# ScalarE sums the moments of the layernorms beside the scans, and the last batch's out_proj weights are loaded early into buffers of u

## The chip, the cores and the metric

The kernel runs on one core of one Trainium2 chip. The metric is the device time of one execution in microseconds. Three runs of the kernel before took 1672.40, 1673.51 and 1674.71 us; the median is 1673.51 us. Its engines are called PE (TensorE), DVE (VectorE), ACT (ScalarE), POOL (GpSimd) and SP (SyncE, which here only issues DMAs). Each engine works through its own instructions in the order in which the program gives them; semaphores make one engine wait for another.

## The reference, cut to what matters

One decoder layer on 4 batches of 512 tokens of width 512: a Mamba block with a selective scan (1024 channels, 16 states each), a cross attention that consists of two SmoothQuant int8 products, and a mixture of 16 experts (top 2) with a shared expert. Each of the three is added to the residual, and each is preceded by a layernorm without weights:

```python
def _layernorm(x, axis=-1, eps=1e-05):
    m = jnp.mean(x, axis=axis, keepdims=True)
    v = jnp.var(x, axis=axis, keepdims=True)
    return (x - m) / jnp.sqrt(v + eps)

def step(h, inputs):                      # the scan, 512 steps
    d_t, B_t, C_t, u_t = inputs
    dA = jnp.exp(d_t[..., None] * A)
    h = h * dA + (d_t * u_t)[..., None] * B_t[:, None, :]
    y = jnp.einsum('bdn,bn->bd', h, C_t)
    return (h, y)

x = x + mamba(_layernorm(x))              # ends with out_proj: einsum('md,bld->blm', out_proj_weight, y)
x = x + quant(_layernorm(x), fside, ctx)
x = x + moe(_layernorm(x))
```

## The kernel before

**The work.** A batch has 4 tiles of 128 tokens. There are three layernorms for each tile, so 4 x 3 x 4 = 48 layernorms of 128 x 512. Each is done by three helpers: `ln_stats` (L327, L328: bn_stats and bn_aggr on DVE give mean and variance), `ln_scale` (L335 to L337: three operations of 128 x 1 on POOL give 1/sqrt(v + eps) by a power, and minus the mean times that) and `ln_scaled` (L341: one ACT activation applies both to the tile).

**The scans.** A batch has 8 groups of 128 channels (`c`), and each group 8 units (`n`), so a batch has 64 slots and the kernel 256. In a slot ACT makes two exponentials of 128 x 512 (L663, into one of two PSUM buffers `da`), POOL one product `bu` of 128 x 1024 (L665, two buffers), DVE the scan over 128 x 1024 (L672) and the product with C (L678), and PE sums over the states into `py` (L690). DVE's L712 multiplies by the gate and writes the result over `u`, which is what out_proj reads; the group is then entered in `self.done` as ("gated", b, c). The `rep` copies (L650, SP) spread delta and delta times u over the partitions for L663 and L665.

**What runs beside them.** Three generators give the rest of the work in steps, each step a few instructions:

- `front(b)` for batches 1 to 3: `layernormed` (first layernorm and transposes), in_proj, convolution, gates, x_proj. All fronts must be over before the scans of batch 3 begin.
- `back(b)`: the out_proj weights `wout` are loaded (L730, eight DMAs of 256 KB, two to a step, into a pool of their own), then the tiles of `x` (L737); out_proj (L742), the addition to `x` (L752), the second layernorm; two quantized products (`quant_linear`); the addition (L787), the third layernorm; `moe_front` with routing (L1110) and the shared expert (L1052, L1060, L1084), whose last addition is L1090. The backs of the four batches follow one another in one generator. Batch 2's back may start only when all fronts are done, so with slot 192; batch 3's needs its own scans and runs after them, apart from its first six channel groups of out_proj, which need only ("gated", 3, 5).
- `experts(group 0)`, the experts for the tokens of batches 0 and 1: sorting, then up to 31 tiles, each with two gathers issued by POOL (L1175 weights, L1419 tokens), transposes (L346), products (L1450, L1465) and a store (L1473). They begin with batch 3's scans and go on after them, beside batch 3's back. The second group begins after batch 3's routing and ends the kernel.

**The planner.** The order of every engine's instructions is fixed when the program is built. `Pace` keeps a modelled time for each engine. In each slot `scan_batch` calls `more` three times: before the scan, between scan and product, and after it. Each call offers every generator two steps. A step is written if the tiles and engines that the generator named with its last `yield` are free by the model, with some tolerance. A generator that lags behind its due count gets a larger tolerance, LATE = 100 ns for each step that it is late; the due count is BACK_STEPS, or FRONT_STEPS, for every DUE = 58 slots. After the scans a loop writes whichever generator is ready first, with a preference for the back.

```python
BACK_STEPS, FRONT_STEPS, DUE, LATE = 164, 112, 58, 100
backs.due = lambda slot: BACK_STEPS * (slot - NC * NU) / DUE
def go_if_clear(self, due=0):
    if not self.over and self.pace.clear(self.wait, max(0, due - self.written) * LATE):
        self.go()
```

`staged(items, *stages)` pipelines: in one step the stages of several items are written, the latest stage first, so that item t is in stage s while item t+1 is in stage s-1. One more stage makes the pipeline one step longer.

**Buffers of u.** The pool `us` holds 17 buffers of 128 x 512 under the tag "u", given out in turn. Batch 0 takes 8, batch 1 takes 4 (its other 4 lie elsewhere), batches 2 and 3 take 8 each; the end of the kernel takes more of them for the results. A tile that gets an old buffer waits until the last reader of that buffer is through.

Of the kernel before, what the change touches and what calls it, by code (L numbers as in the profile page):

```python
# [19 lines left out]
P = 128  # L20
# [22 lines left out]

BACK_STEPS, FRONT_STEPS, DUE, LATE = 164, 112, 58, 100
FIRST = 2000
# [224 lines left out]
class Kernel:  # L270
    def __init__(self, ctx, tc, args):
# [24 lines left out]
        nc.sync.dma_start(self.gate_sb, self.gatew)  # L296
        T = B * NT
        self.idf = const.tile([P, T, 2], F32, name="idf")
        self.topw = const.tile([P, T, 2], F32, name="topw")

# [14 lines left out]
        self.last = None  # L315
        self.ws = {}
        self.skips, self.u_of = {}, []
        self.started = set()
        self.table = False

    def ln_stats(self, x):
# [35 lines left out]
    def layernormed(self, b, sb, bank, xnT):  # L359

        nc = self.nc
        xs, ln, tp = {}, {}, {}

        def load(t):
            xs[t] = sb.tile([P, DM], F32, name="xin", bufs=4)
            nc.sync.dma_start(xs[t], self.x[b, t * P : (t + 1) * P, :])

        def stats(t):
            ln[t] = self.ln_stats(xs[t])
            return ln[t]  # L370

        def scale(t):
            ln[t] = self.ln_scale(ln[t])
            return ln[t]

        def scaled(t):
            self.ln_scaled(xs[t], xs[t], ln[t])
            return xs[t]

        def turn(t):  # L380
            tp[t] = bank.take([P, NK, P])
            self.transposes(tp[t], xs[t], NK)
            return tp[t]

        def turned(t):
            nc.scalar.copy(xnT[:, :, t * P : (t + 1) * P], tp[t])
            bank.done(tp[t])

        for t in range(NT):
            load(t)  # L390
        yield xs[0]
        yield from staged(range(NT), stats, scale, scaled, turn, turned, bank=bank)

# [323 lines left out]
    def back(self, b, G):  # L717
# [6 lines left out]
        with ExitStack() as outer:  # L724
            keep = outer.enter_context(tc.tile_pool(name=f"keep{b}", bufs=1, reuse_waits="tile", side="right"))
            xn = keep.tile([P, NT, DM], F32, name="xn")
            with tc.tile_pool(name=f"out{b}", bufs=2, reuse_waits="tile", side="right") as sb:
                wout = sb.tile([P, NC, DM], F32, name="wout", bufs=1)
                for c in range(NC):
                    nc.sync.dma_start(wout[:, c, :], self.wout[:, c, :])  # L730
                    if c % 2:
                        yield
                xr, po, ln = {}, {}, {}

# [4 lines left out]
                def product(t):  # L739
                    po[t] = G.take([P, DM])  # L740
                    for c in part:
                        nc.tensor.matmul(  # L742
                            po[t],
                            st["u"][c][:, t * P : (t + 1) * P],
                            wout[:, c, :],
                            start=(c == part[0]),
                            stop=(c == part[-1]),
                        )
                    return po[t]

                def added(t):
                    nc.vector.tensor_add(xr[t], xr[t], po[t])  # L752
                    G.done(po[t])

                def stats(t):
                    ln[t] = self.ln_stats(xr[t])
                    return ln[t]

                def scale(t):
                    nc.sync.dma_start(self.x1[b * NT + t], xr[t])  # L760
                    ln[t] = self.ln_scale(ln[t])
                    return ln[t]

                def scaled(t):
                    self.ln_scaled(xn[:, t, :], xr[t], ln[t])

# [5 lines left out]
                if b == B - 1:  # L772
                    part = range(NC - 2)
                    yield PE, wout, lambda: ("gated", b, part[-1]) in self.done
                    yield from G.staged(range(NT), product, added)
                    part = range(NC - 2, NC)
                yield PE, wout, lambda: ("gated", b, NC - 1) in self.done
                yield from G.staged(range(NT), product, added, stats, scale, scaled)
                self.done.add(("out_proj", b))
            with tc.tile_pool(name=f"quant{b}", bufs=2, reuse_waits="tile", side="right") as sb:  # L780
                ln = {}

# [6 lines left out]

                def stats(t):  # L790
                    nc.sync.dma_start(self.x2[b * NT + t], xr[:, t, :])
                    ln[t] = self.ln_stats(xr[:, t, :])
                    return ln[t]

                def scale(t):
                    ln[t] = self.ln_scale(ln[t])
                    return ln[t]

                def scaled(t):
                    self.ln_scaled(xn[:, t, :], xr[:, t, :], ln[t])  # L800
                    return xn
# [20 lines left out]
                yield xr, EW  # L822
                yield from staged(range(NT), add, stats, scale, scaled, store)
            yield from self.moe_front(b, G, xn)
# [328 lines left out]
    def experts(self, sb, group, bank, ahead):  # L1153
# [9 lines left out]
        if sb is not self.last:  # L1163
            fixed = self.sort_fixed(sb, group)
        place = lambda: (self.last, 8) if self.last else (sb, ahead)
        pos = sb.tile([P, T, 2], U32, name=f"pos{group}", bufs=1)
# [552 lines left out]
```

## Time and profile before

The profiled execution took 1669.61 us; its span from the first to the last instruction is 1667.9 us.

| | |
|---|---|
| median of three runs | 1673.51 us |
| profiled execution, and its span | 1669.61 us, 1667.9 us |
| busy: DVE, PE, POOL, ACT | 1220.5, 1216.4, 1125.6, 895.6 us |
| scans (L672), 256 of 2288 ns | 585.8 us on DVE |
| products with C (L678), 256 of 1219 ns | 312.0 us on DVE |
| bu (L665), 256 of 2357 ns | 602.0 us on POOL |
| exponentials (L663), 512 of 691 ns | 352.9 us on ACT |
| bn_stats and bn_aggr (L327, L328), 48 each | 41.4 us on DVE |
| the three POOL operations (L335 to L337), 48 each | 51.6 us on POOL |
| first and last start of a scan | 89.7 and 1341.6 us |
| granted PE clock, mean | 0.851 |

Busy time is what an engine spent in instructions; it says nothing on whether the end waited for it. For that one looks at a stretch: how far each engine is filled there, and what the fullest one waited for. In the lists of waits a row reads "who waited, for whom: total us, times, longest". In rows by line, three figures are the shortest, the median and the longest duration in ns. In a timeline the columns are the start in us, the length in us, engine and line, and in brackets the idle time before and what ended it.

### The profile page before, as it was taken

The page shows a single profiled execution, that of the slowest core. Times are in us where ns is not written, and L with a number is a line of the kernel's source. Part 1 is how long each engine was busy: PE and PEld are TensorE (multiplying, and loading weights), DVE is VectorE, ACT ScalarE, POOL GpSimd, SP SyncE. Part 2 cuts the span into 40 slices and gives each one's busy share as a digit, 9 for nine tenths or more (in the row PEclk, how much of TensorE's full clock was granted, in tenths as well). Part 3 has the DMA queues.
Part 4 walks back from the last instruction along what each step waited for, and adds up shares of the span by engine and source line. Part 5 has one row for each costly group of instructions (what it writes and reads, how often), then busy time and mean ns, then how long its engine had stood idle before and what let it go on. Part 6 is the DMA issues. An engine that isn't in the chain of part 4 may idle for free. (4 is left out here: it accounts for less than half of the span.)

```text
span 1667.9 us, 15571 instructions
## 1 busy us (share of the span) xinstructions
PE 1216.4 (73%) x4552; PEld 585.6 (35%) x4552; DVE 1220.5 (73%) x1322; ACT 895.6 (54%) x1448; POOL 1125.6 (67%) x904
## 2 busy tenths in 40 slices
PE   6867588649676759799776985875656897668980
PEld 2222122103242323233433432363434346434760
DVE  4377899998898896789887998988777933453312
ACT  2365677654668764654886652478654313530330
POOL 1176999887788894777887874878887544027454
PEclk9988789768787978799988897987797999768995
DMA  5564464565463463675443758535577472158957
GB/s 204 150 160 111 98 148 95 125 150 148 106 123 67 110 167 107 152 194 155 91 106 88 194 126 292 139 105 146 146 212 207 123 299 105 52 204 295 360 207 221
DMA packets 109657, 262.21 MB, mean 157 GB/s; under 512 B 16192, under 2 KB 20416, under 8 KB 109504
## 3 DMA queue, kind: packets, MB, share of 16 engines
q1 hardware_dynamic: 93120, 204.50, 46.7%
q0 software_dynamic: 16448, 56.65, 9.8%
q8 instruction: 40, 0.66, 0.2%
q14 instruction: 49, 0.40, 0.1%
HBM read 168.55 MB, written 45.88 MB: 129 GB/s over the span
## 5 line engine op out<-in xcount | busy, mean ns | idle before, releaser
L665 POOL TENSOR_TENSOR bu<-bc,rep 128x1024 f32<-128x1024 f32 x256 | 602.0, 2357 | 171.2 <-DVE da L672 130.5
L672 DVE TENSOR_TENSOR_SCAN da<-da,bu 128x1024 f32<-128x1024 f32 x256 | 585.8, 2288 | 81.2 <-POOL bu L665 60.3
L663 ACT ACTIVATE da<-rep,a_sb 128x512 f32<-128x512 f32 x512 | 352.9, 691 | 298.8 <-DVE h L678 261.5
L678 DVE TENSOR_TENSOR h<-da,bc 128x1024 f32<-128x1024 f32 x256 | 312.0, 1219 | 15.6 <-PE py L690 5.1
L690 PE MATMUL py<-h,sel 128*32 128x512 f32 x1024 | 172.2, 673 | 68.5 <-DVE h L678 68.4
L1175 POOL DMA_INDIRECT wx<-in_wexp,wrow x62 | 62.9, 1015 | 92.6 <-PE bank L1465 29.0
L400 PE MATMUL bank_a<-xnT,win 128*128 128x512 f32 x176 | 91.2, 666 | 12.9 <-DVE gz L357 8.3
L456 POOL TENSOR_TENSOR u<-u,tap 128x511 f32<-128x511 f32 (+2 forms) x72 | 91.2, 1266 | 9.2 <-ACT tap L452 6.7
L690 PEld LDWEIGHTS py<-h,sel 128*32 128x32 f32 x1024 | 30.6, 116 | 187.3 <-DVE h L678 109.9
L400 PE MATMUL bank_g<-xnT,win 128*128 128x512 f32 x176 | 90.0, 659 | 4.4 <-DVE gz L357 2.1
L1419 POOL DMA_INDIRECT xs<-xn_d,tok x62 | 64.0, 1032 | 19.7 <-issue 15.2
L400 PE MATMUL bank_b<-xnT,win 128*128 128x512 f32 x128 | 64.0, 646 | 17.1 <-ACT sp_r L623 17.1
L400 PEld LDWEIGHTS bank_a<-xnT,win 128*128 128x128 f32 x176 | 36.5, 215 | 62.8 <-issue 48.1
L634 POOL TENSOR_TENSOR sp_e<-sp_e,dd 128x512 f32<-128x512 f32 x32 | 40.6, 1270 | 26.2 <-ACT dd L629 26.0
L400 PEld LDWEIGHTS bank_g<-xnT,win 128*128 128x128 f32 x176 | 36.3, 214 | 59.3 <-issue 48.8
L335 POOL TENSOR_SCALAR ln_scale<-ln_mv 128x1 f32<-128x1 f32 x48 | 11.0, 229 | 61.6 <-DVE ln_mv L328 58.5
L686 PE MATMUL py<-u,skip 128*128 128x512 f32 x64 | 37.5, 671 | 13.5 <-DVE u L712 13.5
L1213 POOL DMA_INDIRECT yg<-y_d,pos x32 | 32.5, 1014 | 21.3 <-DMA y_d<-ys 9.3
L400 PEld LDWEIGHTS bank_b<-xnT,win 128*128 128x128 f32 x128 | 26.4, 212 | 52.9 <-issue 29.4
L1223 DVE SCALAR_TENSOR_TENSOR xr<-yg,topw,xr 128x512 f32<-128x512 f32 x32 | 23.8, 751 | 28.4 <-DMA yg<-y_d,pos 27.8
L640 POOL TENSOR_TENSOR dd<-dd,u 128x512 f32<-128x512 f32 x32 | 40.6, 1269 | 1.5
L636 POOL TENSOR_TENSOR sp_e<-sp_e,sp_r 128x512 f32<-128x512 f32 x32 | 40.6, 1268 | 1.4
(404 smaller groups left out, 2386.4 us busy)
## 6 DMA issues: line engine op xcount, KB each, us to landing
rep<-dd SPq DMA_DIRECT2D x128, 512.0 KB
win<-in_win SPq DMA_DIRECT2D x64, 256.0 KB
x<-xr SPq DMA_DIRECT2D x48, 256.0 KB
xr<-x SPq DMA_DIRECT2D x48, 256.0 KB
y_d<-ys SPq DMA_DIRECT2D x48, 256.0 KB
bc<-rows_d SPq DMA_DIRECT2D x32, 256.0 KB
gz_d<-gz SPq DMA_DIRECT2D x32, 256.0 KB
gzl<-gz_d SPq DMA_DIRECT2D x32, 256.0 KB
```

The lines of the kernel that those rows point to most:

```text
L400: nc.tensor.matmul(pj, win[:, k, :], xnT[:, k, :], start=(k == 0), stop=(k == NK - 1))
L456: nc.gpsimd.tensor_add(u[:, j:], u[:, j:], v[j][:, j:])
L634: nc.gpsimd.tensor_sub(e, e, du)
L636: nc.gpsimd.tensor_add(e, e, r)
L640: nc.gpsimd.tensor_mul(du, delta, st["u"][c])
L663: nc.scalar.activation(da[:, i, :], rep[:, i, 0, :], AF.Exp, scale=self.a_sb[:, q, g : g + 1])
L665: nc.gpsimd.tensor_mul(bu, st["bc"][0, g].unsqueeze(1).to_broadcast([P, NP, L]), rep[:, :, 1, :])
L672: self.nc.vector.tensor_tensor_scan(daf, daf, buf, 0.0, ALU.mult, ALU.add)
L678: self.nc.vector.tensor_mul(h, st["da"].pop((c, n)), st["bc"][1, g].unsqueeze(1).to_broadcast([P, NP, L]))
L690: nc.tensor.matmul(py[q * CH : (q + 1) * CH, :], self.sel, st["h"][c, g, q // NP][:, q % NP, :], start=False, stop=(g == NG - 1),)
L1175: nc.gpsimd.indirect_dma_start(out=ws[s], out_offset=None, in_=self.wexp, in_offset=bass.IndirectOffsetOnAxis(ap=wrow[:, s : s + 1], axis= ...
L1419: nc.gpsimd.indirect_dma_start(out=xs[s], out_offset=None, in_=xn_d, in_offset=bass.IndirectOffsetOnAxis(ap=tok[:, s : s + 1], axis=0), bo ...
```

## The change

1. The layernorms get a second form. A new helper `ln_stages` returns the stages of a layernorm for `staged`: with `fast` the old three (stats, scale, last), otherwise five: a sum on ACT (`ln_sum`), minus the mean on POOL (`ln_mean`), the sum of squares of x minus the mean on ACT (`ln_square`), the scale on POOL (`ln_scale_of`), and the old `ln_scaled`. ACT's two passes take their sums from the accumulated output of an activation; the activation's own result goes to one bf16 tile `junk` that nothing reads. The fast form remains for batch 0's first layernorm and for batch 3's second and third.
2. In out_proj the store of the sum to `x1` becomes a stage of its own. In the quantized part the store to `x2` stays with the first stage (`keep_sum`).
3. Batch 3 has no `wout` pool of its own. When batch 2's out_proj is written, eight buffers of u are taken and filled with the eight parts of the weights, two to a step.
4. The experts of group 0 yield the tiles of `sort_fixed` (constants made on POOL) before they go on.
5. BACK_STEPS goes from 164 to 169, FRONT_STEPS from 112 to 114.

```diff
-BACK_STEPS, FRONT_STEPS, DUE, LATE = 164, 112, 58, 100
+BACK_STEPS, FRONT_STEPS, DUE, LATE = 169, 114, 58, 100
...
+        self.junk = const.tile([P, DM], BF16, name="junk")
...
-        self.ws = {}
+        self.ws, self.wout_last = {}, []
...
+    def ln_sum(self, x):
+        total = self.small.tile([P, 2], F32, name="ln_total", bufs=8)
+        self.nc.scalar.activation(self.junk, x, AF.Copy, accum_out=total[:, 0:1])
+        return total
+
+    def ln_mean(self, total):
+
+        self.nc.gpsimd.tensor_scalar_mul(total[:, 0:1], total[:, 0:1], -1.0 / DM)
+
+    def ln_square(self, x, total):
+        self.nc.scalar.activation(self.junk, x, AF.Square, bias=total[:, 0:1], accum_out=total[:, 1:2])
+
+    def ln_scale_of(self, total):
+        nc = self.nc
+        scale = self.small.tile([P, 2], F32, name="ln_scale", bufs=8)
+        nc.gpsimd.tensor_scalar(scale[:, 0:1], total[:, 1:2], 1.0 / DM, EPS_LN, ALU.mult, ALU.add)
+        nc.gpsimd.tensor_tensor(scale[:, 1:2], scale[:, 0:1], self.mhalf, ALU.pow)
+        nc.gpsimd.tensor_mul(scale[:, 0:1], total[:, 0:1], scale[:, 1:2])
+        return scale
+
+    def ln_stages(self, x, scaled, fast):
...
+        return (stats, scale, last) if fast else (sum_of, mean, square, scale_of, last)
...
     def layernormed(self, b, sb, bank, xnT):
...
-        yield from staged(range(NT), stats, scale, scaled, turn, turned, bank=bank)
+        yield from staged(range(NT), *self.ln_stages(xs.get, scaled, b == 0), turn, turned, bank=bank)
...
     def back(self, b, G):
...
-                wout = sb.tile([P, NC, DM], F32, name="wout", bufs=1)
-                for c in range(NC):
-                    nc.sync.dma_start(wout[:, c, :], self.wout[:, c, :])
-                    if c % 2:
-                        yield
+                wout = self.wout_last
+                if b < B - 1:
+                    both = sb.tile([P, NC, DM], F32, name="wout", bufs=1)
+                    wout = [both[:, c, :] for c in range(NC)]
+                    for c in range(NC):
+                        nc.sync.dma_start(wout[c], self.wout[:, c, :])
+                        if c % 2:
+                            yield
...
-                yield from G.staged(range(NT), product, added, stats, scale, scaled)
+                yield PE, *wout, lambda: ("gated", b, NC - 1) in self.done
+                ln = self.ln_stages(xr.get, scaled, b == B - 1)
+                yield from G.staged(range(NT), product, added, ln[0], store, *ln[1:])
                 self.done.add(("out_proj", b))
+                if b == B - 2:
+
+                    for c in range(NC):
+                        self.wout_last.append(self.us.tile([P, DM], F32, name="wout_c", tag="u"))
+                        nc.sync.dma_start(self.wout_last[c], self.wout[:, c, :])
+                        if c % 2:
+                            yield
...
-                yield from staged(range(NT), add, stats, scale, scaled, store)
+                ln = self.ln_stages(lambda t: xr[:, t, :], scaled, b == B - 1)
+                yield from staged(range(NT), add, keep_sum, *ln[1:], store)
...
         if sb is not self.last:
             fixed = self.sort_fixed(sb, group)
+            yield fixed
```

More of the change, by code (lines that the diff above doesn't have):

```diff
@@ L319, in __init__, with put, last, stats @@
         self.table = False
+    def ln_sum(self, x):
[14 more added lines that the diff above has]
+    def ln_stages(self, x, scaled, fast):
+        ln = {}
+        def put(t, value):
+            ln[t] = value
+            return value
+        def last(t):
+            return scaled(t, ln[t])
+        def stats(t):
+            return put(t, self.ln_stats(x(t)))
+        def scale(t):
+            return put(t, self.ln_scale(ln[t]))
+        def sum_of(t):
+            return put(t, self.ln_sum(x(t)))
+        def mean(t):
+            self.ln_mean(ln[t])
+            return ln[t]
+        def square(t):
+            self.ln_square(x(t), ln[t])
+            return ln[t]
+        def scale_of(t):
+            return put(t, self.ln_scale_of(ln[t]))
+        return (stats, scale, last) if fast else (sum_of, mean, square, scale_of, last)
     def ln_stats(self, x):
@@ L361, in layernormed @@
         nc = self.nc
-        xs, ln, tp = {}, {}, {}
+        xs, tp = {}, {}
         def load(t):
@@ L366, in load, with scaled @@
             nc.sync.dma_start(xs[t], self.x[b, t * P : (t + 1) * P, :])
[L368 to L377, printed above, removed]
+        def scaled(t, scale):
+            self.ln_scaled(xs[t], xs[t], scale)
             return xs[t]
@@ L727, in back @@
             with tc.tile_pool(name=f"out{b}", bufs=2, reuse_waits="tile", side="right") as sb:
-                wout = sb.tile([P, NC, DM], F32, name="wout", bufs=1)
-                for c in range(NC):
-                    nc.sync.dma_start(wout[:, c, :], self.wout[:, c, :])
-                    if c % 2:
-                        yield
-                xr, po, ln = {}, {}, {}
+                wout = self.wout_last
[6 more added lines that the diff above has]
+                            yield
+                xr, po = {}, {}
                 def load(t):
@@ L744, in product @@
                             st["u"][c][:, t * P : (t + 1) * P],
-                            wout[:, c, :],
+                            wout[c],
                             start=(c == part[0]),
@@ L753, in added, with store, scaled @@
                     G.done(po[t])
[L755 to L759, printed above, removed]
+                    return xr[t]
+                def store(t):
                     nc.sync.dma_start(self.x1[b * NT + t], xr[t])
[L761 to L765, printed above, removed]
+                def scaled(t, scale):
+                    self.ln_scaled(xn[:, t, :], xr[t], scale)
                 for t in range(NT):
@@ L773, in back @@
                     part = range(NC - 2)
-                    yield PE, wout, lambda: ("gated", b, part[-1]) in self.done
+                    yield PE, *wout, lambda: ("gated", b, part[-1]) in self.done
                     yield from G.staged(range(NT), product, added)
                     part = range(NC - 2, NC)
-                yield PE, wout, lambda: ("gated", b, NC - 1) in self.done
-                yield from G.staged(range(NT), product, added, stats, scale, scaled)
+                yield PE, *wout, lambda: ("gated", b, NC - 1) in self.done
+                ln = self.ln_stages(xr.get, scaled, b == B - 1)
+                yield from G.staged(range(NT), product, added, ln[0], store, *ln[1:])
                 self.done.add(("out_proj", b))
+                if b == B - 2:
[4 more added lines that the diff above has]
+                            yield
             with tc.tile_pool(name=f"quant{b}", bufs=2, reuse_waits="tile", side="right") as sb:
-                ln = {}
                 def load(t):
@@ L788, in add, with keep_sum, scaled @@
                     return xr
-                def stats(t):
+                def keep_sum(t):
                     nc.sync.dma_start(self.x2[b * NT + t], xr[:, t, :])
[L792 to L800, printed above, removed]
+                    return ln[0](t)
+                def scaled(t, scale):
+                    self.ln_scaled(xn[:, t, :], xr[:, t, :], scale)
                     return xn
```

## The prediction

> **What bounds the kernel now.** I read the busy table by stretches first, then VectorE's waits, then the rows of the lines that the change touches, then the timeline around the end of the scans. The stretches below are the four batches of scans; they end when the first scan of the next batch starts.
>
> ```profile
> core 0: us, PE busy (x) PEld busy (x) DVE busy (x) ACT busy (x) POOL busy (x), PEclk, DMA share, GB/s
> 89.70:363.70 274.00, 187.54 (x524) 61.30 (x524) 244.62 (x176) 182.67 (x272) 233.71 (x158) 0.81 0.55 121
> 363.70:682.10 318.40, 234.08 (x796) 101.30 (x800) 269.08 (x258) 202.38 (x321) 244.97 (x185) 0.83 0.51 124
> 682.10:1003.10 321.00, 267.87 (x911) 118.81 (x904) 276.61 (x265) 212.83 (x336) 253.53 (x183) 0.91 0.55 138
> 1003.10:1345.10 342.00, 238.14 (x1060) 128.72 (x1059) 287.11 (x314) 181.65 (x299) 242.28 (x195) 0.84 0.59 167
> sum 1255.40, PE 927.63 PEld 410.12 DVE 1077.42 ACT 779.53 POOL 974.48; mean PE 231.91 PEld 102.53 DVE 269.36 ACT 194.88 POOL 243.62
> ```
>
> DVE is busy for 1077.4 of 1255.4 us (86%), POOL for 78%, ACT for 62%. DVE's 256 scans and 256 products with C come to 898 us (page: 585.8 + 312.0), so about 180 us of its stream is other work that delays the next scan directly. What DVE waits for in the same stretch:
>
> ```profile
> DVE da L672 <- POOL bu L665: 60.3, 22, 27.4
> DVE da L672 <- ACT da L663: 20.6, 17, 5.7
> ...
> DVE ln_stats L327 <- POOL xr L787: 5.5, 3, 2.3
> ...
> DVE ln_stats L327 <- DMA xin<-in_x: 5.2, 1, 5.2
> ```
>
> 27.4 us of the first row lie before the first scan. So while scans run, POOL costs DVE 33 us and ACT 21 us: DVE's own stream sets the pace, POOL is the nearest behind it. After 1345 us come 323 us without scans: the last batch's chain (out_proj, two quantized products, routing, sort, experts).
>
> **The moments, 36 of the 48.** The fast form (VectorE) stays for batch 0's first layernorm and both of batch 3: 12 items of 128 rows. The other 36 lie within the scans. The rows by line, in that stretch:
>
> ```profile
> L327 DVE BATCH_NORM_STATS2 ln_stats<-xr x24: 667/682/697, 412.3 to 1242.1; 128x6 f32<-128x512 f32 x24
> ...
> L327 DVE BATCH_NORM_STATS2 ln_stats<-xin x12: 660/684/697, 93.9 to 661.5; 128x6 f32<-128x512 f32 x12
> ...
> L328 DVE BATCH_NORM_AGGREGATE ln_mv<-ln_stats x36: 181/182/183, 94.6 to 1242.8; 128x2 f32<-128x6 f32 x36
> ```
>
> Off DVE: 36 x (0.683 + 0.182) = 31.1 us. The stalls in front of these lines (5.5 + 5.2) go too, since ACT now waits there; part will reappear at the next DVE instruction that needs late data, so I count half: 5.
>
> On ACT: a sum and a square per item. Nearest rows: a Copy with constants, 128x512 from SBUF, 0.630 us (L627); an activation with one per-partition operand, 0.691 (L663). What the accumulated output adds, no row shows. From below: nothing, it rides along, 36 x 1.32 = 47.5 us. From above: each pass doubled, 95 us. I take a small extra step of 0.2 us each, like the smallest ACT row (0.23 us, 128x68, L1126): 62 us. ACT then stands at 842 of 1255, 67%. All of it lies beside DVE while ACT's exponentials are on time: ACT idled 261 us in front of them only because DVE had not freed the buffer. Where passes bunch, the next scan is late. DVE waited 20.6 us for 780 us of ACT work; 8% more work and longer queues: 4 us lost, between 0 and 20 (those waits doubled).
>
> Here a rule stands against the change. The Trainium skill, "ScalarE: Activation LUTs", Rules for kernel authors, gives adds and multiplies to VectorE; from its section on ACT_TABLE_LOAD (0.186 us + 0.833 ns per element, 0.093 per pointer operand) I estimate 0.61 + 0.71 us per item on ACT, beside DVE's 0.865 in this trace. By that rule the item becomes dearer: if ACT set the end, 36 x 1.32 = 47.5 us more. By the busy row, ACT has 476 us free and DVE 178, so what counts is the 31.1 that leaves DVE. I follow the row. The page's Table sets section lists relu, copy, identity and abs for every set, but not square. A reload is 1.283 us in the trace (L632); two per item would be 92 us. I take none, since Copy, Identity, Abs and Relu ran here without a load and the page gives Square the same precision budget; 92 is the other end.
>
> On POOL: before, 0.221 + 0.567 + 0.264 = 1.05 us per item (L335, L336, L337). After, a mean (as L335), a scale step (as L335), the power, and a product (0.198, L866): 1.21. So 36 x 0.155 = 5.6 us more busy. What matters more: POOL runs in order, and an item now stops it twice for ACT, before once for DVE:
>
> ```profile
> POOL ln_scale L335 <- DVE ln_mv L328: 13.9, 4, 8.1
> ```
>
> A second stop of that size is 14 us more of idle POOL. Behind it waits bu (L665), and behind bu the scan. POOL has slack: it idled 130.5 us in 72 places (1.8 us each) for the scan to free a bu buffer. A third reaching DVE is 5 us. Ends: 0 (all in slack) and 40 (second rival).
>
> **The last batch's weights.** Eight transfers of 256 KB leave the start of the tail and are issued after batch 2's out_proj, in four pairs, inside the scans. What they and the transfers behind them cost today:
>
> ```profile
> 1345.65 3.86 SPq L730 DMA_DIRECT2D wout<-in_wout  x8
> 1349.58 2.92 SPq L737 DMA_DIRECT2D xr<-in_x  x4
> 1349.70 5.39 PE L742 MATMUL bank_a<-wout,u 128*128 128x512 f32 x12 [0.32 <-PE py L690]
> 1359.43 0.69 DVE L752 TENSOR_TENSOR xr<-xr,bank_a 128x512 f32<-128x512 f32 x1 [8.76 <-DMA xr<-in_x]
> ```
>
> The first products start when the last scan sums release PE, not when weights land; PE's own waits for wout there add up to 1.0 us. DVE waits 8.8 us for xr, queued behind wout on SP, but PE doesn't (same columns as the first table):
>
> ```profile
> 1350.00:1387.00 37.00, 37.00 (x132) 19.90 (x131) 11.27 (x25) 5.06 (x10) 17.36 (x25) 1.00 0.84 325
> ```
>
> PE is busy for all of those 37 us, at a clock of 1.00, with out_proj and group 0's experts between. So the early weights are mostly hidden already. Bounds: 1 us (PE's wait) and 9 (DVE's wait, if order follows it); I take 3. If batch 2's chain were done several slots before the scans end, the first six chunks (48 of 64 matmuls of 0.44 us, 21 us) could also go under the scans; today it ends within the last slots (its last add L1090 starts at 1344.5).
>
> In the scans, SP issues eight more transfers (0.43 us each, 3.5 us), ahead of batch 2's quantization weights and later rep copies. The same bursts at 369, 741 and 1011 us have no wait for rep within 20 us behind them: nothing, at worst one such wait (6.7 us, at 1265). The buffers were last read by out_proj of batches 1 and 2, so SP waits for nothing long. Waiting for the sort's constants (yield fixed) takes away one DVE wait of 1.3 us (mk for iota_e): below what I count.
>
> **More steps per batch.** The planner's step counts go from 164 to 169 (back) and 112 to 114 (front), and batch 2 gets four more for the loads. Counting scans, fronts end at slot 175 of the 192 they have: free. Batch 2's back takes slots 192 to 254 of 256, 2.6 steps per slot; nine more are 3.4 slots, two of them free, 1.4 x 5.3 us = 7 us past the scans. In the tail no scans stand between steps; I take 4, from 0 to 16 (slots lost with no cover).
>
> **Sum.** -31 - 5 + 4 (ACT) + 5 (POOL) + 4 (steps) - 3 (weights) = -26 us. The profiled execution took 1669.6 us (span 1667.9), so 1643.6; the median shown is 3.9 above it, so **1647.5** there, taken as 1648. PE work does not change.
>
> **Rivals.**
> - The gain is half lost on batch 2's chain. Its 62 slots take 331 us, and if latency rather than DVE sets them, batch 3 gives none of its 6.9 us and ends up to 16 us late in the tail: -26 + 6.9 + 12 (16 instead of 4) = -7, 1667. For it: DVE idles 55 us in that batch. Against it: the steps are bound to three checks per slot.
> - Slower, by POOL's queue. Each of 36 items holds POOL at the mean until ACT has summed; bu has 1.8 us of slack. A hold of w costs DVE 36 x (w - 1.8). Without holds the sum is -31, so it decides from w = 2.7 us; at w = 2.9 it is +9, 1682. For it: POOL did wait up to 8.1 us at this line, and the planner lets a late back write steps 3 to 5 us before their inputs. Against it: it held POOL only 4 times in 36. Table loads for Square would end on this side too (+66).
> - More than forecast: the tail's first part slides under the scans (-21) and stalls do not reappear: 1622. Against it: batch 2's end.
>
> **How the numbers follow.** Forecast 0.52; half lost 0.18, mostly a small gain; slower 0.22; more 0.08. What the measurement can tell from no change is about 0.2% (3.3 us; the three runs lie within 2.3). So faster 0.70 (forecast, more, and 0.10 of half lost), same 0.07, slower 0.23. The range reaches from 1628, which holds costs of nothing on ACT, POOL and steps and 9 us for the weights, to 1680, most of the slower case's near side; beyond are 0.07 and 0.12. The likeliest case's own range is 1636 to 1660.
>
> **What would show it.** Right: the four stretches shrink by about 6, 9, 7 and 5 us; DVE's busy time falls by 31, ACT's rises by 48 to 95, and L327 stays with 12 items; the waits of L672 for L665 and L663 grow by less than 10 us together. The tail from the last scan stays within 5 us of 323. Wrong: waits of POOL for ACT in the new lines that run to 30 us or more with L672 waiting for L665 beside them, loads of tables in front of Square, or batch 2's shared-expert products running on past the last scan.

## The result, and the profile after

The changed kernel took 1661.22 us (median of 18 runs, 1655.70 to 1667.34) where the kernel before took 1671.42 (18 runs): a ratio of 0.994, 95% interval 0.9927 to 0.9952, so 10.2 us are gained where 26 were forecast (1661.2 against 1647.5, with a likeliest range of 1636 to 1660). A second measurement (e17 below) gave 0.9933 [0.9911, 0.9956]. The profiled execution took 1661.86 us, with a span of 1659.9.

The busy table of the changed kernel by stretches; each ends where the next batch's first scan starts, the last one 3.5 us behind the start of the last scan, as in the table of before:

```profile
core 0: us, PE busy (x) PEld busy (x) DVE busy (x) ACT busy (x) POOL busy (x), PEclk, DMA share, GB/s
90.70:353.50 262.80, 178.47 (x524) 60.21 (x524) 237.89 (x159) 192.90 (x304) 234.64 (x166) 0.82 0.59 126
353.50:671.90 318.40, 225.25 (x788) 101.31 (x788) 261.00 (x233) 225.45 (x379) 252.02 (x202) 0.82 0.51 123
671.90:998.60 326.70, 270.92 (x915) 119.00 (x916) 270.61 (x250) 216.05 (x358) 248.92 (x186) 0.89 0.54 137
998.60:1338.50 339.90, 237.73 (x1007) 124.95 (x1006) 278.47 (x294) 188.11 (x324) 238.53 (x199) 0.82 0.59 166
sum 1247.80, PE 912.37 PEld 405.47 DVE 1047.97 ACT 822.51 POOL 974.12; mean PE 228.09 PEld 101.37 DVE 261.99 ACT 205.63 POOL 243.53
```

DVE lost 1077.4 - 1048.0 = 29.4 us of work, almost the 31.1 of the forecast. The stretch lost only 7.6 us (1255.4 to 1247.8). The rest became idle time of DVE; its waits over the scans (who waited, for whom: us, times, longest):

```profile
POOL bu L711 <- DVE da L718: 140.2, 78, 10.3
DVE da L718 <- POOL bu L711: 74.4, 29, 27.4
DVE da L718 <- ACT da L709: 29.4, 17, 4.4
...
POOL ln_scale L339 <- ACT junk L334: 9.0, 8, 2.3
...
POOL ln_total L331 <- ACT junk L326: 4.4, 2, 2.3
```

The scan (now L718) waits for `bu` 74.4 us instead of 60.3, and for the exponentials 29.4 instead of 20.6: 23 us of waits more, where under 10 had been named as a sign that the forecast was right. POOL's waits in the new lines are short, 13.4 us in all against 13.9 for the old line, so no queue stands behind them.

Nor are the shares of the batches those of an evenly unloaded engine. They shrank by 11.2, 0, -5.7 and 2.1 us (from first scan to first scan; the last to its last scan), where 6, 9, 7 and 5 had been forecast. Most of batch 0's 11 us are one stall that went: before, the 17th scan had waited 8.58 us for `bu`, and that for a late `rep` copy. Batch 1 has such a stall now (the first line is from the timeline of before, the others from the changed kernel's: start, length, engine, line, and in brackets the idle time and what ended it):

```profile
169.77 2.30 DVE L672 TENSOR_TENSOR_SCAN da<-da,bu 128x1024 f32<-128x1024 f32 x1 [8.58 <-POOL bu L665]
...
460.93 7.81 SPq L696 DMA_DIRECT2D rep<-dd  x4
468.11 0.69 ACT L709 ACTIVATE da<-rep,a_sb 128x512 f32<-128x512 f32 x1 [9.59 <-DMA rep<-dd]
...
470.02 4.65 POOL L711 TENSOR_TENSOR bu<-bc,rep 128x1024 f32<-128x1024 f32 x2 [9.12 <-DMA rep<-dd]
472.40 2.30 DVE L718 TENSOR_TENSOR_SCAN da<-da,bu 128x1024 f32<-128x1024 f32 x1 [11.64 <-POOL bu L711]
```

The stall of batch 0 follows the order of the instructions, not DVE's load. It stands at the same scan, 8.5 to 9.7 us long, in all ten kernels of this study with the old layernorms, also in e1 below, where DVE has less to do; it is missing in all ten that plan the new form. Batch 0 takes 273 to 280 us in the first ten and 261 to 263 in the others.

Where the span's 8.0 us come from, by landmarks in us (starts of the first and last scan, end of batch 2's last shared-expert addition, the instruction near the end of batch 3's routing that writes the experts' numbers, called "routing" from here on, and the end of the span):

| | first scan | last scan | batch 2's back ends | batch 3's routing | end |
|---|---|---|---|---|---|
| before | 89.7 | 1341.6 | 1345.2 | 1489.3 | 1667.9 |
| after | 90.7 | 1335.0 | 1341.2 | 1479.0 | 1659.9 |

The scans end 6.6 us earlier, batch 2's back only 4.0. Another 6.3 us come from the stretch between that and the routing (144.1 to 137.8), and 2.3 are given back behind the routing. In the changed kernel batch 2's back ends 6.2 us behind the start of the last scan (before: 3.6), with the last batch's out_proj behind it:

```profile
1334.99 2.29 DVE L718 TENSOR_TENSOR_SCAN da<-da,bu 128x1024 f32<-128x1024 f32 x1
...
1337.19 0.73 DVE L1137 SCALAR_TENSOR_TENSOR xr<-bank_g,sg,xr 128x512 f32<-128x512 f32 x1
1337.83 0.74 DVE L1137 SCALAR_TENSOR_TENSOR xr<-bank_a,sg,xr 128x512 f32<-128x512 f32 x1
1340.48 0.75 DVE L1137 SCALAR_TENSOR_TENSOR xr<-bank_b,sg,xr 128x512 f32<-128x512 f32 x1 [0.78 <-PE bank_b L1131]
...
1341.68 1.91 SPq L786 DMA_DIRECT2D xr<-in_x  x4
...
1343.53 5.42 PE L791 MATMUL bank_b<-wout_c,u 128*128 128x512 f32 x12
```

So two questions were put to the chip: what is a microsecond of DVE worth, and what does the chain of batch 2's back cost?

### The profile page after: what moved, and what is told of

The parts are those of the page before. It is cut to its first block, busy times and chain, and to the rows that moved or that the text cites. A ratio compares the mean times of both kernels' runs of the same rounds, so it can differ in the third digit from the quotient of the medians.

```text
span 1659.9 us, 15722 instructions
## 1 busy us (share of the span) xinstructions
PE 1207.7 (73%) x4552; PEld 584.8 (35%) x4552; DVE 1193.2 (72%) x1250; ACT 941.3 (57%) x1592; POOL 1130.7 (68%) x940
## 5 line engine op out<-in xcount | busy, mean ns | idle before, releaser
L718 DVE TENSOR_TENSOR_SCAN da<-da,bu 128x1024 f32<-128x1024 f32 x256 | 586.2, 2290 | 105.2 <-POOL bu L711 74.4
L736 PE MATMUL py<-h,sel 128*32 128x512 f32 x1024 | 166.1, 687 | 50.2 <-DVE h L724 50.1
L446 PE MATMUL bank_g<-xnT,win 128*128 128x512 f32 x192 | 100.2, 670 | 8.6 <-ACT tap L498 6.0
L446 PE MATMUL bank_b<-xnT,win 128*128 128x512 f32 x160 | 82.1, 661 | 24.6 <-ACT sp_r L669 15.2
L736 PEld LDWEIGHTS py<-h,sel 128*32 128x32 f32 x1024 | 31.1, 119 | 164.4 <-issue 83.3
L446 PE MATMUL bank_a<-xnT,win 128*128 128x512 f32 x128 | 63.2, 640 | 3.0 <-DVE gz L411 2.4
L446 PEld LDWEIGHTS bank_b<-xnT,win 128*128 128x128 f32 x160 | 32.9, 213 | 72.9 <-issue 38.5
L1504 ACT ACTIVATE hs<-bank 128x128 f32<-128x128 f32 x24 | 6.6, 276 | 67.5 <-PE bank L1498 36.5
L791 PE MATMUL bank_b<-wout,u 128*128 128x512 f32 x64 | 36.1, 724 | 10.7 <-ACT tap L498 6.2
L1498 PE MATMUL bank<-xT,wx 128*128 128x128 f32 x352 | 43.1, 276 | 0.6 <-issue 0.6
L1498 PEld LDWEIGHTS bank<-xT,wx 128*128 128x128 f32 x352 | 41.3, 192 | 4.3 <-issue 3.5
L411 DVE SCALAR_TENSOR_TENSOR hs<-hs,bank 128x128 f32<-128x128 f32 x24 | 6.8, 284 | 50.1 <-ACT hs L1504 35.7
```

The lines of the kernel that those rows point to most:

```text
L446: nc.tensor.matmul(pj, win[:, k, :], xnT[:, k, :], start=(k == 0), stop=(k == NK - 1))
L718: self.nc.vector.tensor_tensor_scan(daf, daf, buf, 0.0, ALU.mult, ALU.add)
L736: nc.tensor.matmul(py[q * CH : (q + 1) * CH, :], self.sel, st["h"][c, g, q // NP][:, q % NP, :], start=False, stop=(g == NG - 1),)
L1498: nc.tensor.matmul(ph[:, i, :], w[:, o : o + P], xT[:, k, :], start=(k == 0), stop=(k == NK - 1))
```

## Experiments

Times are medians; each ratio is to the kernel before on the same chip. The chips differ: the kernel before took 1672 us on two of those used and 1654 to 1658 on three others. With one and the same order of instructions there, the part behind the routing took 178.6 us on the one kind (before) and 166.4 on the other (e5). So ratios, or times on one chip, are compared; landmarks up to the routing are set side by side, each from one profiled execution. e1, e2 and e6 compute with altered moments, and for them 50 tiles of experts ran instead of 48. Behind the routing this shows no cost (178.1 us in e1, 165.9 in e6), and up to the last scan the number of products is the same.

### At the order of before: what is an engine's time worth?

The first three kernels keep every instruction of before where it is, and change only how long some of them take, or add the passes without telling the planner.

**e1**, the statistics of the 36 items over 32 columns (DVE relieved, nothing else):

```diff
-        nc.vector.bn_stats(stats, x)
+        nc.vector.bn_stats(stats, x if fast else x[:, :32])
```

> The kernel before in its own order of instructions, with bn_stats of the 36 layernorms within the scans over 32 of the 512 columns (the moments are then those of 32 columns). DVE loses 36 x about 0.58 = 21 us and nothing is added elsewhere. Theory A (DVE sets the pace; what was lost was lost to the time that the new passes take on ACT and POOL): 17 to 21 us faster than before. Theory B (DVE's time is not worth its length, since other waits of the scans fill what is freed): 5 to 11 us faster.

Measured 1666.1 against 1671.96 us, ratio 0.9967 [0.9949, 0.9985]: -5.9 us. The stretch from 90 us to the last scan, of before and then of e1:

```profile
90.00:1341.60 1251.60, 924.13 (x3275) 408.52 (x3276) 1073.62 (x1005) 778.79 (x1224) 973.54 (x718) 0.85 0.55 139
```

```profile
90.00:1335.60 1245.60, 922.70 (x3275) 408.60 (x3276) 1056.92 (x1006) 780.13 (x1228) 976.65 (x719) 0.84 0.56 140
```

DVE's work is 16.7 us shorter, the stretch 6.0. **A microsecond off the fullest engine is worth about a third of one** (by the interval of the ratio, between 0.15 and 0.5).

**e5**, both passes of ACT added to the old form, their cost kept from the planner (`extra` marks what writes `junk`); **e6**, the same with e1's edit, which makes it the shift of the moments from DVE to ACT at an unchanged order, but for a part: bn_stats and bn_aggr stay in short form, so 17 of the 31 us leave DVE:

```diff
         nc.vector.bn_aggr(mv, stats)
+        if not fast:
+            total = small.tile([P, 2], F32, name="ln_total", bufs=8)
+            nc.scalar.activation(self.junk, x, AF.Copy, accum_out=total[:, 0:1])
+            nc.scalar.activation(self.junk, x, AF.Square, bias=self.mhalf, accum_out=total[:, 1:2])
```

> The kernel before in its own order, bn_stats on VectorE as it was, and in addition the change's two ACT passes right behind each of the 36 layernorms' moments, with results that nothing reads. ACT gains 36 x 1.7 = 62 us, nothing else changes. The prediction's costing (ACT has room): 4 us slower than before, at most 8. Theory C (the scans are a ring of engines that wait for one another; a microsecond more or less on any of them is worth a third to a half): 15 to 30 us slower.

> As the run with added passes, and bn_stats over 32 columns, so that DVE loses 18 us: the change's shift of work from DVE to ACT, in the order of the kernel before (the moments are those of 32 columns). Prediction's costing: 12 us faster than before (16 off DVE, 4 back on ACT). Theory C: 8 to 25 us slower; then the gain of the changed kernel comes from its other order and not from the shift.

e5: 1.0041 [1.0022, 1.0061], e6: 1.0032 [1.0018, 1.0047]. The same stretch, of e5 and then of e6:

```profile
90.00:1349.60 1259.60, 923.79 (x3275) 407.08 (x3276) 1074.50 (x1006) 831.41 (x1372) 976.34 (x719) 0.84 0.55 139
```

```profile
90.00:1347.70 1257.70, 923.87 (x3275) 409.37 (x3276) 1056.37 (x1005) 828.70 (x1368) 973.62 (x718) 0.84 0.55 138
```

ACT, busy for 62% of the scans, is 53 us fuller in e5, and the scans are 8 us longer. Taking 17 to 18 us off DVE beside it (e6) brings back 2 of them, which is within the noise. As far as e6 carries it out, the shift loses about 5 us at a fixed order. e5 lies at the upper end of the prediction's costing and short of Theory C, e6 between the two. (The first scans of these profiled executions start at 89.7 to 92.1 us; counted from there, the scans took 8.2 us less than before in e1, 5.5 more in e5 and 6.0 more in e6.) "DVE sets the pace" is refuted. I read the waits as those of a ring: DVE, ACT and POOL pass two buffers of `da` and two of `bu` round, and each one's work delays the others. For POOL that is not shown; no run shortened its work.

**e2**, the mirror image of e1: the changed kernel and its exact order, the ACT passes over 32 columns.

```diff
-        self.nc.scalar.activation(self.junk, x, AF.Copy, accum_out=total[:, 0:1])
+        self.nc.scalar.activation(self.junk[:, :32], x[:, :32], AF.Copy, accum_out=total[:, 0:1])
```

(and so for Square; the planner goes on charging 512 columns)

> The changed kernel in its own order of instructions, with the sum and the square of the 36 layernorms over 32 columns. ACT loses 36 x about 0.85 = 31 us of its 62 and nothing else changes. Theory A: 18 to 25 us faster than before, as ACT no longer delays the exponentials and the deltas. Theory B: 8 to 12 us faster, as the changed kernel is.

1647.16 us, 0.9854 [0.9829, 0.9879]: 14 us below the changed kernel's ratio. From the first to the last scan, of the changed kernel and then of e2:

```profile
90.70:1335.00 1244.30, 908.87 (x3224) 403.95 (x3225) 1044.47 (x929) 822.51 (x1363) 973.85 (x750) 0.84 0.56 139
```

```profile
89.70:1324.70 1235.00, 904.91 (x3224) 405.68 (x3225) 1044.34 (x928) 795.12 (x1363) 973.76 (x750) 0.84 0.56 140
```

With 27 us less on ACT the scans took 1235.0 instead of 1244.3 us, again a third. The remaining 5 us lie behind the last scan and are not explained. By its total of 25 us below before, e2 lies where Theory A put it, while e1 lies where Theory B did: neither holds for both. In this order the passes on ACT cost more for each microsecond (14 us for 27, or 9 in the scans) than in the order of before (8 for 53, e5).

### The parts, each re-planned

**e3** loads the last batch's weights in the tail, as before; **e4** is before with the early weights alone; **e7** is before with the two counts alone; **e8** is the changed kernel with the counts of before.

```diff
 e3
-                if b < B - 1:
+                if True:
...
-                if b == B - 2:
+                if False:
 e7
-BACK_STEPS, FRONT_STEPS, DUE, LATE = 164, 112, 58, 100
+BACK_STEPS, FRONT_STEPS, DUE, LATE = 169, 114, 58, 100
 e8
-BACK_STEPS, FRONT_STEPS, DUE, LATE = 169, 114, 58, 100
+BACK_STEPS, FRONT_STEPS, DUE, LATE = 164, 112, 58, 100
```

(e4 takes from the change the lines with `wout` and `wout_last`, and nothing else. So e3 and e8 differ from e7 and e4 not by the moments alone: they also have the store of `x1` as a stage and the experts' `yield fixed`.)

> The changed kernel with the last batch's out_proj weights loaded where they were before, at the start of the tail. Theory A and B both: 7 to 10 us faster than before, since the weights were all but hidden. Rival W (the gain is that of the weights): within 3 us of before.

> The kernel before with the early weights alone, moments on DVE. Theory A and B: 0 to 3 us faster. Rival W: 7 to 10 us faster. Another order of the planner may move each of these by a few us.

> The kernel before with the step counts 169 and 114 alone: no work is changed, only the planner's order. It shows how much an order is worth. If orders are worth little: within 2 us of before. If a large part of the 10 us is order: 3 to 10 us away from before, either way.

> The changed kernel with the old step counts 164 and 112. If orders are worth little: within 2 us of the changed kernel, 10 us faster than before. Else 3 to 10 us away from the changed kernel, more likely slower, as the backs then run later.

| | ratio [95%] | last scan | batch 2's back ends | routing |
|---|---|---|---|---|
| e3 without early weights | 0.9958 [0.9940, 0.9976] | 1341.7 | 1330.9 | 1481.1 |
| e4 early weights alone | 0.9978 [0.9965, 0.9991] | 1342.1 | 1349.5 | 1488.6 |
| e7 counts alone | 0.9921 [0.9894, 0.9948] | 1340.8 | 1313.7 | 1476.6 |
| e8 without the counts | 1.0091 [1.0070, 1.0113] | 1322.8 | 1364.6 | 1498.0 |

e4 agrees with the 3 us of the forecast (4.1): batch 2's back, with four steps of loads more, ends 4.3 us later, and from there to the routing it takes 139.1 us instead of 144.1. e3's gain (8.4 us) lies in its forecast range too, but e7 has more without the moments. The surprise is the pair e7 and e8. **Two constants of the planner, whose steps I had costed at plus 4 us, alone bring 12 us; without them the whole change loses 14.** e8 shows why, in DVE's timeline around the end of the scans:

```profile
1322.77 2.29 DVE L718 TENSOR_TENSOR_SCAN da<-da,bu 128x1024 f32<-128x1024 f32 x1
...
1351.82 0.75 DVE L1137 SCALAR_TENSOR_TENSOR xr<-bank_b,sg,xr 128x512 f32<-128x512 f32 x1 [3.38 <-PE bank_b L1131]
1355.25 0.75 DVE L1137 SCALAR_TENSOR_TENSOR xr<-bank_a,sg,xr 128x512 f32<-128x512 f32 x1 [2.68 <-PE bank_a L1131]
1358.68 0.75 DVE L1137 SCALAR_TENSOR_TENSOR xr<-bank,sg,xr 128x512 f32<-128x512 f32 x1 [2.68 <-PE bank L1131]
1363.86 0.75 DVE L1137 SCALAR_TENSOR_TENSOR xr<-bank,sg,xr 128x512 f32<-128x512 f32 x1 [4.42 <-PE bank L1131]
```

Here the scans are through 19 us earlier than before. But batch 2's back, with nine steps more, ends 42 us behind the start of the last one, 19 us later than before (4 of them are e4's, from the loads), and the last batch's out_proj stands behind it in the same generator. The shorter scans are all lost. The raised counts of the changed kernel buy back 23 us of that chain (1364.6 to 1341.2) for 12 us of scans (1322.8 to 1335.0).

### Other counts

One-line edits: BACK_STEPS of the changed kernel at 180, 190 and 174 (e9, e10, e15), and of before at 180, 190 and 170 (e11, e12, e16).

> The changed kernel with BACK_STEPS 180 instead of 169: by the order of its instructions batch 2's back ends with scan 246 of 256, not behind the last. Theory D (the end is the later of two things, the last scan and the end of batch 2's back, plus a tail that does not change): the scans set the end now, and the chain before batch 3's out_proj is gone: 12 to 25 us faster than before. Theory E (it is only the worth of one order or another): anywhere within 15 us of the changed kernel, with no relation to where batch 2's back ends.

> The changed kernel with BACK_STEPS 190: batch 2's back ends with scan 239, and the first part of batch 3's out_proj is written at scan 242. Theory D: that part (48 matmul records of 0.44 us, 21 us) leaves the tail, so 20 to 40 us faster than before, less what the scans lose to steps that are forced before their inputs are ready. Theory E: as for 180.

> The kernel before with BACK_STEPS 180 alone: batch 2's back ends with scan 241. Theory D: 13 to 30 us faster than before, as much as or more than the whole change gave. Theory E: within 15 us either way.

> The kernel before with BACK_STEPS 190 alone: batch 2's back ends with scan 234. Theory D: 15 to 40 us faster than before; slower than the changed kernel with 190 by what the shift of the moments is worth once the scans set the end (up to 13 us).

> The changed kernel with BACK_STEPS 174, its batch 2's back by scan 251 instead of 255. Theory D: 8 to 20 us faster than before if the scans stay within 10 us of those at 169; slower than before if they stretch as at 180 (80 us).

> The kernel before with BACK_STEPS 170 alone: batch 2's back by scan 249. 169 with 114 gave 13 us. Theory D: 8 to 15 us faster than before; if that gain was the luck of one order: within 5 us of before or slower.

Ratios: e9 1.0368 [1.0334, 1.0402], e10 1.0318 [1.0285, 1.0352], e11 1.0259 [1.0223, 1.0295], e12 1.0573 [1.0535, 1.0612], e15 1.0053 [1.0036, 1.0071], e16 1.0151 [1.0126, 1.0176]. None of the six brought the gain that Theory D forecast, and e9 to e11 left Theory E's 15 us as well. A higher count brought batch 2's back forward in the order of the instructions, but not in time: it ended at 1352 to 1380 us in all six, later than in the kernels that they come from (1341 and 1345), and the last scan started at 1370 to 1466. The scans stop for steps that are written before their data are there. DVE's waits in e9 (columns as above):

```profile
DVE da L718 <- POOL bu L711: 90.1, 33, 27.4
...
DVE xn L1122 <- PE bank_a L1099: 21.4, 5, 8.0
...
DVE xsc L1005 <- PE bank_b L940: 10.1, 2, 9.3
```

In the changed kernel the waits at L1122 add up to 4.2 us, in e9 to 24.4 with the other banks. All of DVE's waits for PE come to 132 us in e9's scans, against 71 in the changed kernel's and 66 before. And two settings of the counts that are one step of the back and two of the front apart move before to -12 us (169 and 114, e7) and to +26 (170 and 112, e16): **the order that the planner happens to find is worth more than either part of the change.**

### The moments without more stages

If the chain of batch 2 is what eats the gain, the moments should gain without additional stages. **e13** has the whole change, but both sums in one stage on ACT, the squares not centred, the mean taken off on POOL, and the counts of before; **e14** is the same with a count of 168.

```diff
+        def sums(t):
+            put(t, self.ln_sum(x(t)))
+            self.ln_square(x(t), ln[t])
+            return ln[t]
...
-        return (stats, scale, last) if fast else (sum_of, mean, square, scale_of, last)
+        return (stats, scale, last) if fast else (sums, scale_of, last)
```

> The changed kernel with both sums of an item taken in one stage on ACT (the squares without the mean, which POOL then takes off) and the x1 store back in the scale's stage, so that a back has no more stages than before, and with the old counts 164 and 112. Batch 2's back is written up to scan 255, as before. Theory D with the steps as the cost (what the change lost, it lost to five more steps per batch): scans end some 10 to 18 us earlier than before and batch 2's back with them, 10 to 20 us faster than before. If the shift from DVE to ACT is itself worth nothing (as in the order of before, where it cost 5 us): within 4 us of before, or slower.

> The same with BACK_STEPS 168: batch 2's back is written by scan 251. Theory D: the scans set the end, at some cost to them: 12 to 25 us faster than before. If a larger tolerance costs the scans as much as at 180: slower than before.

e13: 0.9963 [0.9948, 0.9977]; its last scan starts at 1328.9, batch 2's back ends at 1348.2. Against e8, which has the same counts, this is 13 parts in a thousand (some 21 us) better: the stages do cost. Batch 2's back ends 16.4 us earlier than in e8, and about where it ends in e4 (1349.5), which has the old layernorms. e13 has `yield fixed` as e8 does, so that step is not what made the chain late; the stages are. But e13 is no better than the changed kernel, and against e4 its 1.5 parts in a thousand are within the noise. e14 gave 1.0055 [1.0034, 1.0076]: last scan 1357.5, batch 2's back 1344.7. With the raised count this variant lost.

### The change without the moments

The last pair runs on one chip: **e17** is the changed kernel again, **e18** has its early weights and its counts, but the layernorms of before (e4's edit and e7's together; it lacks the stage for the store and `yield fixed` too).

> The changed kernel itself, beside the next run on one chip. If the ratio of the first measurement holds on this chip: 0.994, 10 us below before. If the chip with the shorter tail changes the share: between 0.990 and 0.998.

> The changed kernel without its first two parts: early weights and the counts 169 and 114 stay, the layernorms have their old form. Theory 'the order decides' (counts alone gave 13 us, weights 4): 13 to 17 us below before, so not above the changed kernel, and the moments on ScalarE are worth nothing beyond the order. Rival 'the moments carry the gain': 4 us below before at most, at least 6 us above the changed kernel. If it is 8 us or more above before, the orders of neighbouring kernels differ by more than the parts and no share can be given to the moments.

| | time | ratio [95%] | last scan | batch 2's back ends | routing |
|---|---|---|---|---|---|
| e17 | 1661.96 | 0.9933 [0.9911, 0.9956] | 1334.8 | 1341.1 | 1482.4 |
| e18 | 1647.44 | 0.9843 [0.9803, 0.9884] | 1340.6 | 1320.3 | 1467.8 |

**Without the moments on ScalarE the kernel is 14.5 us faster than with them** (by the ratios 15, give or take 8), and has the lowest ratio of the study: this version beats both kernels. It lies 25 us below before, beyond the 13 to 17 that had been expected. The end of its scans, from the timeline:

```profile
1319.59 0.75 DVE L1099 SCALAR_TENSOR_TENSOR xr<-bank_b,sg,xr 128x512 f32<-128x512 f32 x1 [2.68 <-PE bank_b L1093]
1320.79 0.88 SPq L740 DMA_DIRECT2D xr<-in_x  x2
...
1322.31 5.32 PE L745 MATMUL bank_g<-wout_c,u 128*128 128x512 f32 x12
...
1327.46 5.31 PE L745 MATMUL bank_a<-wout_c,u 128*128 128x512 f32 x12
...
1335.42 5.42 PE L745 MATMUL bank_b<-wout_c,u 128*128 128x512 f32 x12
...
1340.56 2.29 DVE L672 TENSOR_TENSOR_SCAN da<-da,bu 128x1024 f32<-128x1024 f32 x1
1340.67 5.31 PE L745 MATMUL bank_g<-wout_c,u 128*128 128x512 f32 x12
```

Batch 2's back is over before the last six scans, so out_proj's first six channel groups, 48 records of products, run beside the last scans (the last 12 begin with the last scan): from 1322.3 on, where the changed kernel begins at 1343.5. That is what the early weights are for, and the moments take it away. The moments buy 5.8 us of scans (1340.6 to 1334.8) and cost 20.8 us of the chain (1320.3 to 1341.1), with the same counts and the same loads. At the routing 14.6 us of it are left (1482.4 against 1467.8), and 11.3 at the end of the two profiled executions; the medians differ by 14.5.

## Why the prediction was wrong in size, and its sign right by luck

**The sign came out right by another cause.** The counts, costed as a loss, gain 12 us alone (e7), and the weights 4 (e4); the moments, from which the gain was to come, bring none where they were compared. **Several parts seen one by one were near.** ACT's four records of an item add up to 0.630 + 0.187 + 0.708 + 0.187 = 1.71 us, 61.6 for 36, where 62 had been taken; the rows (shortest, median and longest ns):

```profile
L326 ACT ACTIVATE junk<-xr x24: 612/629/631, 424.5 to 1236.1; 128x512 bf16<-128x512 f32 x24
L326 ACT ACTIVATION_READ_ACCUMULATOR junk<-xr x24: 185/187/190, 425.0 to 1236.6; 128x1 f32 x24
L334 ACT ACTIVATE junk<-xr,ln_total x24: 705/708/727, 435.0 to 1241.5; 128x512 bf16<-128x512 f32 x24
L334 ACT ACTIVATION_READ_ACCUMULATOR junk<-xr,ln_total x24: 185/187/204, 435.7 to 1242.1; 128x1 f32 x24
```

However, each read begins 0.094 us before its pass has ended (median of 72), so the two passes with their reads take 0.72 and 0.80 us, and ACT's busy time rose by only 45.7 us over the span (895.6 to 941.3), near the forecast's lower end of 47.5: that 1.71 agrees with what had been taken is an accident of the sum. Square caused no table load (75 loads before and after). POOL did not become a queue: its new waits are 2.3 us at most, below the 2.7 from which that rival would have decided. The early weights were 3 us by forecast and 4.1 in e4.

**"-31 (DVE)", the largest term, failed.** DVE's busy time fell by 29.4 us as foreseen, but the sum took it at one for one. e1 shows a third, at an unchanged order: some 10 us for the 31 (5 to 16 by its interval). I had read DVE's 86% against POOL's 78% as "sets the pace"; but POOL waited for DVE and DVE for POOL and ACT in the same stretch, and with two buffers each, a scan is late if any of the three is. Nor is the price of DVE's time one number: where the planner finds another order, the moments on ACT brought the last scan forward by 19.3 us (e4 to e8), 13.2 (e4 to e13) and 5.8 (e18 to e17) and not at all from e7 to e3 (0.9 later). The Trainium skill, "Perfetto Trace Analysis", Identifying the Most-Contended Engine, names the engine with the highest occupancy and has it optimized first; here 16.7 us off that engine gave 6.0 (e1), and 27 us off ACT, which is far less full, gave 9.3 in another order (e2), the same third.

**"+4 (ACT)" was too small, and paired with the wrong cover.** e5's 53 us of ACT work lengthened the scans by 8 us; e6 loses 5 us with both, although 17 us had left DVE; had the sum's terms held, it would have gained some 12. The rule that I had set aside (the Trainium skill, "ScalarE: Activation LUTs", Rules for kernel authors, gives adds and multiplies to VectorE) would have had the sign right at this order. The estimate of 0.61 + 0.71 us from that page's section What ACT_TABLE_LOAD costs was near the measured 0.630 + 0.708, without the reading of the accumulators.

**"+4 (steps)", with 16 as its other end, was the mis-sized step on the other side.** At the old counts the nine steps put batch 2's end 19.4 us later (1345.2 to 1364.6, e8). Four of the nine are the moments' stages in batch 2's back, one is the store's, four are the loads'. The five of moments and store put the end of the chain 15.1 us later from e4 to e8, 17.2 from e7 to e3 and 20.8 from e18 to e17; without the stages (e4 to e13) it comes 1.3 earlier. This cost is alike in three orders, where the gain of the scans is not. I read a step as a place in a queue of stages that wait for one another, not as a share of a slot. That the constants themselves change the whole order, and bring 12 us with no other edit (e7), was not in the sum at all.

**The rival "half lost on batch 2's chain"** named the right mechanism, the latency of that chain, and a time of 1667 (-7 us), near the -10.2 measured. That nearness is luck, as the rival had no term for the 12 us of the counts. It had 0.18 of the chance because the chain was seen as limited by checks per slot; what is lost against e18 is the head start of the last out_proj, which the forecast had only as an upside ("the tail's first part slides under the scans").

The parts together, as differences of medians to before in us, each on one chip ("moments" with the store's stage and `yield fixed`):

| counts | neither | early weights | moments | both |
|---|---|---|---|---|
| 164, 112 | 0 | -4 (e4) | not run | +14 (e8) |
| 169, 114 | -12 (e7) | -25 (e18) | -8 (e3) | -10 (e17, after) |

In all three pairs the moments lose: by 4, 15 and 18 us. The first is hardly clear of the noise, and only the second is of one chip. In these orders the gain of the change is that of the counts and the early weights, less the moments.

**Open:** how much of this is the chance of an order. From e7 to e16 the counts differ by one and two steps, and the time by 38 us; no neighbour of e18 was run, and the moments with a planner that charges `bn_stats` what it took (683 ns; it charges by the 6 values written) weren't tried. Nor was it found what differs between the two kinds of chips behind the routing.

## What to carry to other kernels

The busy share names the fullest engine, not the price of its time: where engines pass two buffers round in a ring, measure the price by shortening an instruction at an unchanged order, on the engine that is relieved and on the one that takes the work. Count an edit's stages on the chain that ends last, beside its instructions; here five stages there cost more (15 to 21 us) than the 31 us of instructions saved were worth. And where a planner fixes the order, run its constants alone, with and without the edit, before an edit is credited with a gain.

## What the hardware showed beyond that

An activation with an accumulated output is two instructions: the pass (0.630 us for a Copy of 128x512, as long as the Copy without a sum in the trace of before) and a read of the accumulator of 0.187 us, of which 0.094 lie beside the end of the pass. Much of both does not depend on the size. The rows of e2, over 32 columns:

```profile
L326 ACT ACTIVATE junk<-xr x24: 212/229/231, 423.1 to 1222.1; 128x32 bf16<-128x32 f32 x24
...
L334 ACT ACTIVATE junk<-xr,ln_total x24: 305/308/328, 433.3 to 1228.3; 128x32 bf16<-128x32 f32 x24
```

With the two reads such an item takes 0.72 us (0.32 + 0.40), against 1.52 (0.72 + 0.80) over sixteen times the columns. Small sums on ACT are dear for their size.
